# Layer 0's self-attention: turned probabilities between two projections, copied by one engine, scaled in two halves, and a new order of the first loads

## The chip, the core and the metric

The kernel is one program on one core of a Trainium2 chip. The core has five engines that run their own instruction queues in order and meet at semaphores: TensorE (PE in the profile; PEld is its loading of the stationary operand), VectorE (DVE), ScalarE (ACT), GpSimd (POOL) and SyncE (SP), which here only issues transfers. The metric is the device time of one execution in microseconds (us), as the median of several runs. Beside it stands one profiled execution with its trace; its span is the time from its first to its last instruction.

## What is computed

The reference is a decoder of two layers on 32 sequences of 100 tokens with 256 features, in float32. Each layer is self-attention, cross-attention to a context of 361 rows, and a mixture of experts, each on a layer norm of x and added to x. The change lies in layer 0's self-attention, and that is all that is needed here:

```
xn = layernorm(x)                                # 32 x 100 x 256
q, k, v = xn Wq + bq, xn Wk + bk, xn Wv + bv      # 16 heads of 64
p = softmax(causal(q k^T / 8))                    # 100 x 100 for each head
x = x + (p v) Wo + bo
```

After it come layer 0's cross-attention and experts, and then layer 1.

## The kernel before, in words

**Layout.** x stays in SBUF for the whole kernel: 3,200 rows as 25 tiles of 128 rows (NF = 25, D = 256). A normed and transposed copy, xnT, holds features on the partitions. A sequence has 100 rows, so tiles and sequences do not line up; `pieces` and `tile_of` map one to the other.

**Start.** SP issues, in this order: all of x in seven transfers (L91), the four weights wq, wk, wv, wo of 1 MB each into one tile wA (L243), the biases bqk, bv, bo (L247, L248, L134), and then fills and weight staging in DRAM for later stages (from L1097). SP has one queue, so what stands first goes first.

**Stage.** `l0_attn` runs 64 steps, n = 0 to 63, two for each sequence b, with eight heads each (g = n % 2). Two extra steps drain the pipeline. The order of TensorE's work is written out by hand (`manual_schedule` for PE); the order on the other engines is a scheduler's, which follows the data and its own estimate of times. Ahead of the loop stand `front(0)` and `front(4)` (norm and transposes of tiles 0 to 7), the projections of the first two sequences, and the first values.

In a step TensorE does, in this order:

- `scores(n)`: 8 products q k^T into two PSUM banks (16 matmul records in the profile, out of tiles qk). VectorE then copies the allowed ones into s (masked copy, L310) and takes the negative row maximum m (L312). ScalarE takes 8 exps with row sums rz (L316), VectorE the reciprocal of rz (L319), and GpSimd multiplies e by it, all 100 x 800 elements at once (L320).
- `proj` for q and then for k: an eighth of the projections of the next two sequences, two blocks of each. ScalarE adds q's bias (L287), VectorE k's (L289).
- `turn(n-1)`: 8 transposes of the probabilities of the step before, into two banks, copied out to sT by `evac` (L329).
- `vals(b+1, g)`: half of v for the next sequence; VectorE adds the bias (L297).
- `values(n-1)`: p v from sT and v; ScalarE copies the result to zT (L341).
- every now and then `out`: the output projection of a finished tile of 128 rows, added to x by VectorE (L230) with its norm statistics; in some other steps `front` or `next_norm`: norm and transposes of tiles (L200).

`evac` alternates by a counter that runs through the whole kernel: every second copy goes to ScalarE, the others to VectorE (in layer 1's cross-attention every third to ScalarE). In `turn` the first half goes to VectorE and the second to ScalarE.

All PSUM banks of this stage have one tag with 8 buffers, so each request takes the bank that was asked for eight requests earlier and waits for its readers. A step asks for eight: two for scores, one for q, two for turn, one each for k, v and values; `out`, `front` and `next_norm` ask for more.

In the last steps (n of 60 and more) there are no sequences left to project, so `turn` follows the scores directly.

Of the kernel before, what the change touches and what calls it, by code (L numbers as in the profile page):

```python
# [12 lines left out]
AF = mybir.ActivationFunctionType  # L13
ALU = mybir.AluOpType
AX = mybir.AxisListType

P = 128
NB = 32
T = 100
NT = NB * T  # L20
NF = NT // P
# [23 lines left out]
FRONT0 = {**{f: 4 for f in range(0, 20, 4)}, 20: 5}  # L45
# [32 lines left out]
class Kernel:  # L78
    def __init__(self, ctx, tc, a):
        self.ctx, self.tc, self.nc, self.a = ctx, tc, tc.nc, a  # L80
        nc = tc.nc
        self.n_evac = 0
        self.const = ctx.enter_context(tc.tile_pool(name="const", bufs=1))
        self.wts = ctx.enter_context(tc.tile_pool(name="wts", bufs=1))
        self.lnp = ctx.enter_context(tc.tile_pool(name="ln", bufs=2))
        self.norms, self.norm_of = {}, {}
        self.x = self.const.tile([P, NF, D], F32, tag="x", name="x_sb")
        xd = a["x"].rearrange("b t d -> (b t) d").rearrange("(f p) d -> p f d", p=P)
        for f in range(0, NF, 4):
            n = min(4, NF - f)  # L90
            nc.sync.dma_start(self.x[:, f : f + n, :], xd[:, f : f + n, :])  # L91
        self.xnT = self.const.tile([P, NK, NT], F32, tag="xnT", name="xnT")
        self.ident = self.const.tile([P, P], F32, tag="ident", name="ident")
        make_identity(nc, self.ident)
# [60 lines left out]
        return t  # L155


    def norm_stats(self, f, groups):

        nc = self.nc  # L160
        f0 = max(g for g in groups if g <= f)
        n, i = groups[f0], f - f0
        if i == 0:
            self.norm_of[n] = [
                self.lnp.tile([P, n, *k], F32, tag=f"{tag}{n}", name=tag)
                for tag, k in (("st", [6]), ("mv", [2]), ("rstd", []))
            ]
        st, mv, rstd = self.norm_of[n]
        self.norms[f] = mv[:, i, 0:1], rstd[:, i : i + 1]
        nc.vector.bn_stats(st[:, i, :], self.x[:, f, :])  # L170
        nc.vector.bn_aggr(mv[:, i, :], st[:, i, :])
        if i == n - 1:
            nc.vector.tensor_scalar_add(rstd, mv[:, :, 1], EPS)
            nc.scalar.activation(rstd, rstd, AF.Sqrt)
            nc.vector.reciprocal(rstd, rstd)
# [57 lines left out]
    def l0_attn(self):  # L233
        nc, tc, a = self.nc, self.tc, self.a
        with ExitStack() as st:
# [3 lines left out]
            wq, wk, wv, wo = (w[:, i * 2048 : (i + 1) * 2048] for i in range(4))  # L239
            wq, wk, wv = (v.rearrange("p (k n) -> p k n", k=NK) for v in (wq, wk, wv))  # L240
            wo = wo.rearrange("p (c n) -> p c n", c=8)
            for t, n in ((wq, "wq0"), (wk, "wk0"), (wv, "wv0"), (wo, "wo0")):
                nc.sync.dma_start(t, a[n].rearrange("(k p) n -> p k n", p=P))  # L243
            cp = st.enter_context(tc.tile_pool(name="c0a", bufs=1))
            pool = st.enter_context(tc.tile_pool(name="p0a", bufs=2))
            bqk = cp.tile([P, 2, 8], F32, tag="bqk", name="bqk")
# [2 lines left out]
            nc.vector.tensor_scalar_mul(bqk[:, 0, :], bqk[:, 0, :], 0.125)  # L249
            bv = self.row_bias(cp, a["bv0"], 1024, "bv")  # L250
            bo = self.row_bias(cp, a["bo0"], D, "bo")
            keep = self.tri(cp, "keep", -1, 1, 1.0, 0.0)
            mask = cp.tile([T, T], U32, tag="mask", name="mask")
            nc.vector.tensor_copy(mask, keep)
# [6 lines left out]
            q, k, v, p, sT = {}, {}, {}, {}, {}  # L261
# [3 lines left out]
            def front(f):  # L265

                n = FRONT0[f]
                for i in range(f, f + n):
                    self.norm_stats(i, FRONT0)
                for i in range(f, f + n, 2):  # L270
                    m = min(2, f + n - i)
                    self.norm_turn(i, m, self.norm_rows(i, m, bias=bo), self.bank_m())

            def proj(b0, c, ws, out, s):

                if c == 0:
                    out[b0 // 2] = pool.tile([P, 8, 2 * T], F32, tag=f"qk{s}", name=f"qk{s}")
                t = out[b0 // 2]
                pm = self.bank_m()[:, : 4 * T].rearrange("p (c t) -> p c t", c=2)
                for j in range(2):  # L280
                    self.mm(pm[:, j, :], [
                        (ws[:, i, (c + j) * P : (c + j + 1) * P], self.xn_of(i, b0, 2)) for i in range(NK)
                    ])
                for j in range(2):
                    bias = bqk[:, s, c + j : c + j + 1]
                    if s == 0:
                        nc.scalar.activation(t[:, c + j, :], pm[:, j, :], AF.Identity, bias=bias, scale=0.125)  # L287
                    else:
                        nc.vector.tensor_scalar_add(t[:, c + j, :], pm[:, j, :], bias)  # L289
# [10 lines left out]
            def scores(n):  # L300
                b, g = divmod(n, 2)
                cols = slice((b % 2) * T, (b % 2 + 1) * T)
                s = ss[n % 2]
                ps = [self.bank_s()[:T, : 4 * T].rearrange("p (c t) -> p c t", c=4) for _ in range(2)]
                for c in range(4):
                    for j in range(2):
                        r = slice(64 * j, 64 * j + 64)
                        self.mm(ps[j][:, c, :], [(q[b // 2][r, 4 * g + c, cols], k[b // 2][r, 4 * g + c, cols])])
                for j in range(2):
                    nc.vector.copy_predicated(s[:, 4 * j : 4 * j + 4, :], self.mid(mask, 4), ps[j])  # L310
                m = pool.tile([T, 8], F32, tag="m", name="m", bufs=3)
                nc.vector.tensor_reduce(m, s, AX.X, ALU.max, negate=True)  # L312
                t = p[n] = pool.tile([T, 8, T], F32, tag="e", name="e", bufs=3)
                rz = pool.tile([T, 8], F32, tag="rz", name="rz", bufs=3)
                for i in range(8):
                    nc.scalar.activation(  # L316
                        t[:, i, :], s[:, i, :], AF.Exp, bias=m[:, i : i + 1], accum_out=rz[:, i : i + 1]
                    )
                nc.vector.reciprocal(rz, rz)  # L319
                nc.gpsimd.tensor_tensor(t, t, self.last(rz, T), ALU.mult)  # L320

            def turn(n):
                t = p.pop(n)
                for j in range(2):
                    pt = self.bank_t()[:T, : 4 * T].rearrange("p (c t) -> p c t", c=4)
                    for c in range(4):
                        nc.tensor.transpose(pt[:, c, :], t[:, 4 * j + c, :], self.ident[:T, :T])
                    sT[n, j] = pool.tile([T, 4, T], F32, tag="sT", name="sT", bufs=4)
                    self.evac(sT[n, j], pt)  # L329

            def values(n):
                b, g = divmod(n, 2)
# [10 lines left out]
            def out(b):  # L343

                f = tile_of(b)
                if f is None:
                    return
                self.out_proj(f, wo)
                self.norm_stats(f, HALVES)
                if f in (5, 11, 17):  # L350
                    later.extend(range(f - 5, f, 2))
# [4 lines left out]

            with tc.manual_schedule(engines={mybir.EngineType.PE}):
                front(0)
                front(4)
                for c in range(0, 8, 2):  # L360
                    proj(0, c, wq, q, 0)
                    proj(0, c, wk, k, 1)
                for n in range(2):
                    vals(0, n)
                last = 2 * NB
                for n in range(last + 2):
                    b, g = divmod(n, 2)
                    if n < last:
                        scores(n)
                        b0 = b // 2 * 2 + 2  # L370
                        if b0 < NB:
                            c = 2 * (n % 4)
                            proj(b0, c, wq, q, 0)
                            proj(b0, c, wk, k, 1)
                    if 0 < n <= last:
                        turn(n - 1)
                    if b + 1 < NB:
                        vals(b + 1, g)
                    if 0 < n <= last:
                        values(n - 1)  # L380
                    if g:
                        if b > 0:
                            out(b - 1)
                    elif b % 5 == 4 and b < 20:
                        front(4 * (b + 6) // 5)
                    elif later:
                        next_norm()
# [1582 lines left out]
```

## Time and profile before

| | |
|---|---|
| median of 3 runs | 3237.91 us (3234.86 to 3237.93) |
| profiled execution, its time | 3232.65 us |
| its span | 3230.9 us |
| mean granted TensorE clock | 0.979 |
| head, 0 to 31 us: PE busy | 18.27 us |
| layer 0 self-attention, 31 to 620: PE, DVE, ACT, POOL busy | 559.6, 299.7, 308.0, 114.9 us |
| its steps begin | scores 0 at 31.19, scores 2 at 44.22, scores 60 at 577.56 |
| a plain step in it | 7.45 us; with an output projection 11.10 us |
| layer 0 cross-attention begins | 619.16 us |

How to read it: the page gives the busy time of each engine as a share of the span. A wait is given as engine, result and line, then whom it waited for, and then the total, the count and the longest wait in us. A line of the timeline gives start, duration, engine, line, operation, result and operands, shapes and count; in square brackets stands the idle time of that engine just before, and what ended it. Instructions of one kind that follow each other are merged into one line, so a gap inside such a line is seen only in its length. ps_t is a PSUM bank, whatever it holds. `x16` for scores are 8 products with two records each.

### The profile page before, as it was taken

To read this page: it belongs to the slowest core of one execution; us is meant where nothing else is said; L and a number is where in the kernel's file an instruction comes from. 1 tells how busy PE (TensorE), PEld (TensorE's weight loads), DVE (VectorE), ACT (ScalarE), POOL (GpSimd) and SP (SyncE) were. 2 spreads that over 40 slices of the span, in tenths; PEclk is the share of its full clock that TensorE was granted. 3 is DMA by queue.
4 is the path that set the end of the run, shared out by engine and by line. 5 is a ranking of instruction groups with operands and counts; after the bars stand their busy time and mean duration, and the time that the engine had idled before them with its cause. 6 is when DMAs were issued, how large, how long until landed. Compare 5 with 4: busy or idle time off the path is not lost. (4 is left out here: it accounts for less than half of the span.)

```text
span 3230.9 us, 67902 instructions
## 1 busy us (share of the span) xinstructions
PE 3076.5 (95%) x26832; PEld 2234.8 (69%) x26832; DVE 1773.6 (55%) x4565; ACT 1412.5 (44%) x4407; POOL 912.2 (28%) x984
## 2 busy tenths in 40 slices
PE   8999999899999999999997999999999999999983
PEld 6777777566666657888884677777777777776662
DVE  5555545466766742222225776667666676665442
ACT  4554555466566531122122225555555555555120
POOL 2211211255555543000006330011212112122474
PEclk9999999899999999999998999999999999999996
DMA  9830000000000022554452000000000000000486
GB/s 316 305 133 1 1 1 1 13 14 14 14 14 14 7 96 100 182 203 178 176 213 75 15 5 6 6 30 27 21 12 10 11 10 13 7 11 13 138 202 187
DMA packets 122440, 225.86 MB, mean 70 GB/s; under 512 B 40541, under 2 KB 98837, under 8 KB 115328
## 3 DMA queue, kind: packets, MB, share of 16 engines
q1 hardware_dynamic: 93600, 127.32, 12.3%
q0 software_dynamic: 27792, 90.81, 8.7%
q8 instruction: 215, 3.52, 0.5%
q10 hardware_dynamic: 720, 3.28, 0.2%
q14 instruction: 113, 0.93, 0.1%
HBM read 153.77 MB, written 113.61 MB: 83 GB/s over the span
## 5 line engine op out<-in xcount | busy, mean ns | idle before, releaser
L1628 POOL DMA_INDIRECT x_d<-xr,slot x200 | 194.4, 972 | 786.3 <-DVE kT L124 243.4
L425 ACT ACTIVATE wBx<-ps_t,m 100x361 f32<-100x361 f32 x512 | 281.0, 560 | 261.0 <-DVE m L422 238.6
L595 DVE TENSOR_REDUCE m<-ps_t 100x1 f32<-100x361 f32 x512 | 240.1, 525 | 109.6 <-PE ps_t L129 108.7
L129 PE MATMUL ps_t<-xnT,wA 128*128 128x200 f32 x1536 | 287.2, 337 | 3.0 <-DMA wA<-in_wq 1.5
L129 PEld LDWEIGHTS ps_t<-xnT,wA 128*128 128x128 f32 x1536 | 259.7, 190 | 38.7 <-issue 17.5
L422 DVE TENSOR_REDUCE m<-ps_t 100x1 f32<-100x361 f32 x512 | 241.4, 525 | 78.9 <-PE ps_t L129 76.9
L129 PE MATMUL ps_t<-xT,w 128*128 128x256 f32 x1276 | 283.2, 381 | 0.7 <-ACT xT L123 0.7
L129 PEld LDWEIGHTS ps_t<-xT,w 128*128 128x128 f32 x1276 | 240.0, 190 | 41.7 <-issue 9.3
L320 POOL TENSOR_TENSOR e<-e,rz 100x800 f32<-100x800 f32 x64 | 97.4, 1522 | 456.2 <-DVE rz L319 450.9
L129 PE MATMUL ps_t<-wA,cT 128*121 128x512 f32 x384 | 186.9, 598 | 5.3 <-DVE kT L124 5.3
L616 ACT ACTIVATE e<-ps_t 121x300 f32<-121x300 f32 x512 | 173.2, 431 | 41.7 <-PE ps_t L129 41.7
L129 PE MATMUL ps_t<-kT,qT 64*100 64x361 f32 x1024 | 190.2, 488 | 0.9 <-ACT wBx L425 0.9
L129 PE MATMUL ps_t<-cT,wA 128*128 128x361 f32 x512 | 189.8, 495 | 1.3 <-DVEq L1228 1.3
L316 ACT ACTIVATE e<-s,m 100x100 f32<-100x100 f32 x512 | 186.1, 365 | 5.9 <-DVE m L312 5.5
L434 PEld LDWEIGHTS ps_t<-ident,wBx 100*121 100x121 f32 x1536 | 178.3, 186 | 12.6 <-issue 5.5
L129 PE MATMUL ps_t<-wA,zT 128*128 128x256 f32 x800 | 185.4, 385 | 0.0
L434 PE MATMUL ps_t<-ident,wBx 100*121 100x100 f32 x1536 | 185.4, 270 | 0.0
L620 POOL TENSOR_TENSOR es<-e 121x400 f32<-121x400 f32 x128 | 132.6, 1036 | 177.6 <-ACT e L616 177.5
L1310 DVE TENSOR_TENSOR h<-ps_t,g 128x256 f32<-128x256 f32 x145 | 61.2, 424 | 199.4 <-ACT g L1309 199.4
L129 PEld LDWEIGHTS ps_t<-wA,zT 128*128 128x128 f32 x800 | 150.8, 192 | 28.4 <-issue 3.5
L124 DVE COPY eT<-ps_t 121x300 f32<-121x300 f32 x340 | 146.9, 461 | 31.3 <-PE ps_t L434 27.9
L452 PE MATMUL ps_z<-eT,v 121*64 121x100 f32 x3072 | 160.3, 253 | 0.0
(301 smaller groups left out, 5776.6 us busy)
## 6 DMA issues: line engine op xcount, KB each, us to landing
x_d<-fill SPq DMA_DIRECT2D x16, 1284.0 KB
we<-in_wexp SPq DMA_DIRECT2D x32, 384.0 KB
cT<-in_ctxT SPq DMA_DIRECT2D x64, 181.5 KB
xe<-x_d SPq DMA_DIRECT2D x32, 321.0 KB
xe_d<-zero SPq DMA_DIRECT2D x8, 1024.0 KB
xe<-xe_d SPq DMA_DIRECT2D x29, 256.0 KB
y_d<-y SPq DMA_DIRECT2D x29, 256.0 KB
w_d<-in_wg SPq DMA_DIRECT2D x16, 320.0 KB
```

The source lines that it names most:

```text
L124: return self.nc.vector.tensor_copy(out, in_)
L129: self.nc.tensor.matmul(out, lhsT=l, rhs=r, start=(i == 0), stop=(i == n - 1))
L316: nc.scalar.activation(t[:, i, :], s[:, i, :], AF.Exp, bias=m[:, i : i + 1], accum_out=rz[:, i : i + 1])
L320: nc.gpsimd.tensor_tensor(t, t, self.last(rz, T), ALU.mult)
L422: lay.after = nc.vector.tensor_reduce(m, ps[i], AX.X, ALU.max, negate=True)
L425: nc.scalar.activation(t[:, :L], ps[i], AF.Exp, bias=m, accum_out=sums[b][:, h : h + 1])
L434: nc.tensor.transpose(pt[:, c, :], e[n, i][:, c * KC : (c + 1) * KC], self.ident[:T, :T])
L452: nc.tensor.matmul(out, lhsT=v, rhs=eT[n, i][:, c, :], start=first, stop=last)
L595: nc.vector.tensor_reduce(m[:, j, o : o + 1], ps[r], AX.X, ALU.max, negate=True)
L616: nc.scalar.activation(t[:, r], ps[r].rearrange("p (c t) -> p c t", c=NKC), AF.Exp)
L620: nc.gpsimd.tensor_tensor(s, t[:, :, 0, :], t[:, :, 1, :], ALU.add)
L1628: got = nc.gpsimd.indirect_dma_start(out=self.x1_d[:, :], out_offset=bass.IndirectOffsetOnAxis(ap=slot[:, j, k : k + 1], axis=0), in_=xr[: ...
```

## The change

Five edits, all in layer 0's self-attention or ahead of it:

1. Of x, tiles 0 to 3 are loaded first, in two transfers; then wq and wk; then tiles 4 to 7; then the biases; then wv and wo; then the rest of x.
2. The statistics of tiles 4 to 7 may not start before the last normed row of tiles 0 to 3.
3. The scale by the reciprocal row sums is done in two halves of four heads, each with its own reciprocal. The first half can be scaled after four exps, the second after eight.
4. `turn` copies both halves out by VectorE; `evac` and its counter are not used. The counter stands 128 lower after this stage, so every second copy still falls to the same engine later, and every third one does not.
5. In a step, the projection for q comes before `turn` and the projection for k after it.

```diff
-        for f in range(0, NF, 4):
-            n = min(4, NF - f)
+        def load_x(f, n=4):
+            n = min(n, NF - f)
             nc.sync.dma_start(self.x[:, f : f + n, :], xd[:, f : f + n, :])
+        self.load_x = load_x
+        load_x(0, 2)
+        load_x(2, 2)
...
-        nc.vector.bn_stats(st[:, i, :], self.x[:, f, :])
+        got = nc.vector.bn_stats(st[:, i, :], self.x[:, f, :])
+        if after is not None:
+            self.depend(got, [after.ins], "not ahead of the first tiles' norm")
...
-            for t, n in ((wq, "wq0"), (wk, "wk0"), (wv, "wv0"), (wo, "wo0")):
+            for t, n in ((wq, "wq0"), (wk, "wk0")):
                 nc.sync.dma_start(t, a[n].rearrange("(k p) n -> p k n", p=P))
+            self.load_x(4)
...
             bo = self.row_bias(cp, a["bo0"], D, "bo")
+            for t, n in ((wv, "wv0"), (wo, "wo0")):
+                nc.sync.dma_start(t, a[n].rearrange("(k p) n -> p k n", p=P))
+            for f in range(8, NF, 4):
+                self.load_x(f)
...
-                    self.norm_stats(i, FRONT0)
+                    self.norm_stats(i, FRONT0, self.last_row if f == 4 else None)
...
-                for i in range(8):
-                    nc.scalar.activation(
-                        t[:, i, :], s[:, i, :], AF.Exp, bias=m[:, i : i + 1], accum_out=rz[:, i : i + 1]
-                    )
-                nc.vector.reciprocal(rz, rz)
-                nc.gpsimd.tensor_tensor(t, t, self.last(rz, T), ALU.mult)
+                for j in range(2):
+                    h = slice(4 * j, 4 * j + 4)
+                    for i in range(8)[h]:
+                        nc.scalar.activation(
+                            t[:, i, :], s[:, i, :], AF.Exp, bias=m[:, i : i + 1], accum_out=rz[:, i : i + 1]
+                        )
+                    nc.vector.reciprocal(rz[:, h], rz[:, h])
+                    nc.gpsimd.tensor_tensor(t[:, h, :], t[:, h, :], self.last(rz[:, h], T), ALU.mult)
...
-                    self.evac(sT[n, j], pt)
+                    nc.vector.tensor_copy(sT[n, j], pt)
...
                             proj(b0, c, wq, q, 0)
-                            proj(b0, c, wk, k, 1)
                     if 0 < n <= last:
                         turn(n - 1)
+                    if n < last and b0 < NB:
+                        proj(b0, c, wk, k, 1)
```

More of the change, by code (lines that the diff above doesn't have):

```diff
@@ L155, in tri, with norm_stats @@
         return t
-    def norm_stats(self, f, groups):
+    def norm_stats(self, f, groups, after=None):
         nc = self.nc
```

## The prediction

> **What bounds the kernel now.** I read the page first (shares by engine), then busy time by stage, then the waits of TensorE inside the stage that the diff touches, then that stage's timeline step by step.
>
> ```profile
> PE 3076.5 (95%) x26832; PEld 2234.8 (69%) x26832; DVE 1773.6 (55%) x4565; ACT 1412.5 (44%) x4407; POOL 912.2 (28%) x984
> ```
>
> The whole is TensorE-bound. Layer 0's self-attention lies at 31 to 620 us; there PE is busy 559.6 of 589 us. The waits of PE from 31 to 577, and from 577 to 620, are these:
>
> ```profile
> PE ps_t L129 <- ACT sT L123: 18.3, 33, 2.0
> ...
> PE ps_t L327 <- POOL e L320: 7.6, 2, 4.2
> PE ps_t L129 <- DVE sT L124: 1.2, 2, 0.9
> ```
>
> So the only thing the steady steps wait for is ScalarE's copy of turned probabilities. One such step in the timeline:
>
> ```profile
> 304.15 0.85 PE L327 MATMUL ps_t<-ident,e 100*100 100x100 f32 x8
> 304.84 1.88 PE L129 MATMUL ps_t<-wA,xnT 128*100 128x512 f32 x4
> 305.04 0.57 DVE L124 COPY sT<-ps_t 100x400 f32<-100x400 f32 x1
> ...
> 306.57 0.47 ACT L123 COPY sT<-ps_t 100x400 f32<-100x400 f32 x1
> 306.76 0.20 DVE L319 RECIPROCAL rz<-rz 100x8 f32<-100x8 f32 x1 [1.14 <-ACT e L316]
> 307.09 0.71 PEld L129 LDWEIGHTS ps_t<-sT,v 100*64 100x64 f32 x16 [1.21 <-ACT sT L123]
> 307.09 0.91 PE L129 MATMUL ps_t<-sT,v 100*64 100x100 f32 x16 [0.36 <-ACT sT L123]
> ```
>
> The transposes end at 305.0. VectorE copies its half at once, ScalarE its half only at 306.57, after the eighth exp of the next step, which stands ahead of it. The values matmul starts late.
>
> How much in all: start to start, a step's work on PE is scores 0.88, projections 2.81, turn 0.69, values of the next batch 1.81 (579.18 to 580.99, where nothing waits), weighted values 0.84: 7.03 us. The 58 steps from 44.22 to 577.56 take 533.3. Of that 58 x 7.03 = 407.7 is work, 22 output projections x 3.65 = 80.3, norm transposes 9.9 (nine of 0.59, three of 1.01, one of 1.54, read as differences between steps). 35.4 is left. A plain step loses 0.42 (551.56 to 559.01 is 7.45); part of it hides inside matmul groups that read 1.33 long in place of 0.91, so the waits view shows only 18.3. Steps with norm work lose up to 2.0.
>
> **What the Trainium skill says.** "TensorE: Matmul & The Clock Gate", under "Architectural detail": ScalarE and VectorE are strict FIFO. The trace agrees: the copy waited 1.6 us behind exps. Same page, Part 1: after an idle window of about 3.4 us the array runs at half clock until a busy one. The trace agrees:
>
> ```profile
> 584.00:586.00 2.00, 0.00 (x0) 0.00 (x0) 1.05 (x2) 1.18 (x7) 1.35 (x1) 1.00 0.00 0
> 586.00:588.00 2.00, 1.78 (x10) 1.22 (x11) 0.57 (x1) 2.00 (x13) 0.17 (x1) 0.76 0.00 0
> 588.00:590.00 2.00, 2.00 (x3) 0.30 (x2) 0.00 (x0) 0.82 (x4) 0.00 (x0) 0.50 0.00 0
> ```
>
> (columns: stretch, PE, PEld, DVE, ACT, POOL busy, clock, DMA). After 3.44 idle the clock is 0.50. "ScalarE: Activation LUTs", "What ACT_TABLE_LOAD costs": about 1.28 us per load; the trace has 1.28.
>
> **Part 1, copies and order.** Both copies go to VectorE, and the transposes move ahead of the k projection (1.405 us, half of 2.81), so they end at 0.88 + 1.405 + 0.69 = 2.97 us into the step instead of 4.38. VectorE's queue in the built program then is: two masked copies (0.98 to 2.08), max (to 3.07), two sT copies of 0.57 (to about 4.25), k bias add, reciprocal, add, reciprocal, v add. Weighted values stand at 7.03 - 0.84 = 6.19. The copies have 1.9 us to spare; the stall goes: -0.42 in a plain step. The new weight falls on VectorE: +0.57 and one more reciprocal of at most 0.20. Does it become the bound? Its loop: exps run from 3.17 (0.1 after the max) for 8 x 0.363 to 6.07; second reciprocal to 6.4; v add 0.64 to 7.05; next masked copy wanted at 7.03 + 0.98 = 8.0. Spare 0.95. In the steps with norm rows (up to four x 0.36) or a table load (1.28) the copies slip by 1.4 to 1.7, still under 1.9. Banks: eight are taken per step as before, and every bank that PE waits for was freed in the step before. What is late next: nothing; PE itself. I take -33.7 (35.4 less 1.75 below), with +1 for the tightest norm steps.
>
> **Part 2, the scale in halves.** GpSimd, not in the way: 100x800 takes 1.52, a 128x256 add 0.72, so 400 elements are estimated at 0.95 to 1.04. Second half ready at about 6.4 + 1.1 = 7.5; its transposes come at 7.03 + 2.28 + 0.35 = 9.66. Hidden by 2.1 us; uncovered it would cost +0.5 per step. The transposes now carry waits for single exps; the before's step 1 (36.70) carries seven such and turns in 0.73, so at most +0.04 a step if not overlapped, 0 taken. More ACT counting signals: no row, between 0 and +0.02 x 58; 0 taken.
>
> **Part 3, the clock.** At 198 to 201 the clock is 0.50 after a 1.65 us stall on sT; steps 188.27 and 198.72 lose 4.0 together where like steps lose 1.84 and 0.42: 1.75 is clock. Without the stall it should go: -1.75 (0 if it was not the stall).
>
> **Part 4, the tail (577.56 to 619.16).** No projections; PE waits for exps, scale, transposes. The second half of the scale alone is on that chain (-0.5 each time), but VectorE now puts its two sT copies around the max, where ScalarE had the first (+0.9 at two groups of values). By hand, from scores 60 at 0: masked copies to 2.2 (behind an output's add and stats, 1.0), sT to 2.8, max to 3.75, sT to 4.3, values end 5.1 (before 4.27); exps to 6.75, halves scaled at 6.4 and 8.0, turn ends 8.4 (before 9.4); vals, values, output end 14.7 (before 17.3, with 1.65 of half clock: vals 3.53 for 1.88); the next values end 19.9 (20.9), the next turn 23 (27.6), output 28.9 (35.0, half clock again), cross-attention begins 36.0 (41.6). So 5.6 earlier if the clock stays up. Idle pieces of 1 to 3 us remain, and the clock may dip in them as before, so I take about half: -3 (0 to -6).
>
> **Part 5, the head.** SP's order: x 0-3, wq, wk, x 4-7, biases, wv, wo, the rest. Before, x 0-3 are in at 5.07, wq at 15.5, wk at 18.05: 2.55 per 1 MB weight, 364 GB/s for x. Estimated: wq 7.6, wk 10.1, x 4-7 11.6, bq 12.5, x 8-11 20.4, last x 25. But PE's order keeps the transposes of tiles 4-7 ahead of the first projection. Their chain: stats, aggregates (0.39 a tile), with the bias scale queued between and waiting for bq, to 13.9; root and reciprocal 0.5; four rows; transposes 15.2 to 17 or, at half clock after some 6 us idle, 18.5. The 64 projection records (0.1756 each) then end at 28.2 to 30; before they end at 27.66 (1.4 + 0.9 waiting for wq and wk). Stats of tiles 8 to 24 now sit between k bias adds on VectorE, waiting for x; the root of tiles 20-24 sits between the first two groups of exps and costs two more table loads, 2.56, which the next exps start late by, with turn(1) still covered. Zero fills start after x in either order, same bytes ahead. The two smaller x transfers add one DMA to SP, 0.44 to 0.51 of issue, while the queue is full. Whether the array is really cold there the trace of before can't show: its first transposes (430 and 380 ns against 279 later) look cold though the clock reads 1.00. Sum: +2.5 at the start of step 2 (0 warm and early, +5 cold with x late).
>
> **Sum.** -33.7 + 1 - 1.75 - 3 + 2.5 = -35. Later stages keep their work; a different alternation of copies in the last cross-attention changes no wait of PE, which shows none there. Span 3230.9 - 35 = 3196. The profiled execution is 3232.65, 1.75 around the span, and 5.3 under the runs' median 3237.91, so the median becomes 3203.
>
> **Rivals.**
> 1. VectorE takes over: each in-order wait on it adds a bit and the loop grows from 6.1 to 7.25. Then only 0.2 of the 0.42 is won: 58 x 0.22 = 12.8 less: 3216. For: two reciprocals wait for exps with the v add behind. Against: 0.95 spare.
> 2. The head gives back more: x late, half clock through the projections: +10 in place of +2.5: 3211. Against: weights are all in by 10.
> 3. It does not do what it says: PE's time moves into another wait of equal size, such as the earlier transposes for the scale. They come 1.4 sooner. Against: 2.1 spare. About 3238.
> 4. Slower: the same loop on VectorE beyond 7.45, that is 1.3 us over my sum. At 7.7: 58 x 0.25 = 14.5, less the sum's small terms (-2): 3250. For: VectorE does all evacuation but qk and z. Against: its busy time per step is 4.3 + 0.8 of 7.
>
> **How the numbers follow.** Main case 0.70, own range 3193 to 3213 (head, tail and clock at their ends); rival 1 0.13; rival 2 0.08; rival 3 0.04; rival 4 0.05. Faster than 0.2% (6.5 us, what this kernel's runs can tell from no change): 0.91; within: 0.04; slower: 0.05. The range takes in rivals 1 and 2 with their own spread, and at its low end a tail without half clock: 3190 to 3222.
>
> **What would show it.** Right: no wait of PE for sT between 50 and 570; plain steps of 7.03 to 7.07; steps with an output at 10.7; the clock at 1.00 around 198; step 2's scores at 45 to 49; the tail's two clock dips shorter. Wrong: PE waiting for DVE in values or for POOL in turn (rivals 1, 3), masked copies starting later than 1.3 after the scores begin, projections later than 20 us (rival 2).

## The result and the profile after

The changed kernel takes 3204.05 us (median of 5 runs, 3193.76 to 3207.05); the kernel before, beside it, 3237.91. The ratio is 0.990, 95% interval 0.9884 to 0.9916: faster by 1.0%. A later set of runs of both gave 3201.19 against 3236.13, ratio 0.9896 (0.9875 to 0.9916). The forecast was 3203, with 3190 to 3222 around it.

The line of the page with TensorE's share, after:

```profile
span 3202.3 us, 68027 instructions
...
PE 3067.3 (96%) x26832; PEld 2231.9 (70%) x26832; DVE 1813.5 (57%) x4692; ACT 1393.2 (44%) x4346; POOL 925.7 (29%) x1048
```

The same number of matmuls is busy for 9 us less, and the span is 28.6 us shorter: 19 us of idle went, and 9 us by which waits inside a group or a halved clock had stretched matmuls. The waits of PE in the whole of steps 2 to 59 (50.3 to 549.7 us; total, times, longest) are now one line, and it is not about copies:

```profile
PE ps_t L207 <- DVE xn L185: 0.2, 1, 0.2
```

Before, this stretch had 18.3 us of waits for ScalarE's copy. One step in the timeline after, one with an output projection behind the values (start, length, engine and line, operation; PE, VectorE and GpSimd's first half scale):

```profile
313.96 0.95 PE L134 MATMUL ps_t<-qk,qk 64*100 64x100 f32 x16
...
314.85 1.62 PE L134 MATMUL ps_t<-xnT,wA 128*128 128x200 f32 x8
314.95 1.10 DVE L322 COPY_PREDICATED s<-mask,ps_t 100x400 f32<-100x400 uint32 x2 [0.94 <-PE ps_t L134]
316.08 0.99 DVE L324 TENSOR_REDUCE m<-s 100x8 f32<-100x800 f32 x1
...
316.30 0.85 PE L341 MATMUL ps_t<-ident,e 100*100 100x100 f32 x8
...
316.98 1.04 DVE L343 COPY sT<-ps_t 100x400 f32<-100x400 f32 x2
...
319.23 0.85 POOL L334 TENSOR_TENSOR e<-e,rz 100x400 f32<-100x400 f32 x1 [4.86 <-DVE rz L333]
...
320.18 0.91 PE L134 MATMUL ps_t<-sT,v 100*64 100x100 f32 x16
```

Both copies end at 318.02, 4.06 us into the step; the values matmul that reads them starts at 320.18, 6.22 in, with 2.2 to spare and no wait (in the steps with norm rows the room goes down to 0.75). PE is through with it at 321.02, 7.06 after the scores began.

From the same timeline, by the starts of the steps, the change is placed like this (us):

| stretch | before | after | change | predicted |
|---|---|---|---|---|
| start to step 2 | 44.22 | 50.29 | +6.07 | +2.5 |
| steps 2 to 59 | 533.34 | 499.42 | -33.92 | -34.45 |
| step 60 to the cross-attention's first matmul | 41.60 | 38.52 | -3.08 | -3 |
| from there to the end of the span | 2611.7 | 2614.1 | +2.3 | 0 |
| span | 3230.9 | 3202.3 | -28.6 | -35 |

The head is the part that went against the forecast. PE's first projection in the kernel before, and PE's timeline of the head after:

```profile
15.54 1.62 PE L129 MATMUL ps_t<-xnT,wA 128*128 128x200 f32 x8 [1.46 <-DMA wA<-in_wq]
```

```profile
6.87 1.99 PE L207 MATMUL ps_t<-ident,xn 128*128 128x128 f32 x8 [6.87 <-DVE xn L185]
17.09 0.48 PE L207 MATMUL ps_t<-ident,xn 128*128 128x128 f32 x1 [8.23 <-DVE xn L185]
17.82 1.21 PE L207 MATMUL ps_t<-ident,xn 128*128 128x128 f32 x4 [0.26 <-DVE xn L185]
19.28 0.90 PE L207 MATMUL ps_t<-ident,xn 128*128 128x128 f32 x3 [0.26 <-DVE xn L185]
19.98 12.84 PE L134 MATMUL ps_t<-xnT,wA 128*128 128x200 f32 x64
...
44.43 0.55 PE L341 MATMUL ps_t<-ident,e 100*100 100x100 f32 x4 [0.24 <-POOL e L334]
45.88 0.55 PE L341 MATMUL ps_t<-ident,e 100*100 100x100 f32 x4 [0.90 <-POOL e L334]
```

The first projection stands at 19.98 (15.54 before), behind the transposes of tiles 4 to 7, whose rows come late. And step 1 now waits 1.14 us for the two halves of the scale. Of the 6.07 us, 4.99 are there when step 0 begins (36.18 for 31.19), and step 1 adds 1.08 (8.60 for 7.52).

### The profile page after: what moved, and what is told of

Its sections match the earlier page's. It is cut to its first block, busy times and chain, and to the rows that moved or that the text cites. A ratio compares the mean times of both kernels' runs of the same rounds, so it can differ in the third digit from the quotient of the medians.

```text
span 3202.3 us, 68027 instructions
## 1 busy us (share of the span) xinstructions
PE 3067.3 (96%) x26832; PEld 2231.9 (70%) x26832; DVE 1813.5 (57%) x4692; ACT 1393.2 (44%) x4346; POOL 925.7 (29%) x1048
## 5 line engine op out<-in xcount | busy, mean ns | idle before, releaser
L134 PE MATMUL ps_t<-xnT,wA 128*128 128x200 f32 x1536 | 299.4, 339 | 0.6 <-DVE x_sb L237 0.6
L334 POOL TENSOR_TENSOR e<-e,rz 100x400 f32<-100x400 f32 x128 | 109.5, 856 | 414.0 <-DVE rz L333 397.1
L631 ACT ACTIVATE e<-ps_t 121x300 f32<-121x300 f32 x512 | 173.4, 430 | 41.7 <-PE ps_t L134 41.6
L129 DVE COPY eT<-ps_t 121x300 f32<-121x300 f32 x339 | 146.7, 461 | 31.2 <-PE ps_t L449 27.1
```

Source lines behind the costliest of these rows:

```text
L129: return self.nc.vector.tensor_copy(out, in_)
L134: self.nc.tensor.matmul(out, lhsT=l, rhs=r, start=(i == 0), stop=(i == n - 1))
L334: nc.gpsimd.tensor_tensor(t[:, h, :], t[:, h, :], self.last(rz[:, h], T), ALU.mult)
L631: nc.scalar.activation(t[:, r], ps[r].rearrange("p (c t) -> p c t", c=NKC), AF.Exp)
```

## The experiments

Each ratio is against runs of the kernel before on the same chip: its median is 3224.68 us on one chip and 3236 on two others, so medians of different chips are not compared. The starts of the steps come from each run's own profile; "cross-attention" is its first matmul (619.16 before, 588.23 after).

**The copies alone.** The theory to test: the copies carry the gain of the steps. The rival: the place of the transposes does, or the two share it.

```diff
 # kernel before
-                    self.evac(sT[n, j], pt)
+                    nc.vector.tensor_copy(sT[n, j], pt)
```

> The kernel before with one edit: both copies of turned probabilities on VectorE. My theory (the stall is ScalarE's copy standing behind eight exps, and the place of the transposes only adds room): in a plain step the transposes end 4.4 us in, VectorE's two copies run to about 5.5, the values matmul wants them at 6.19, so plain steps come down from 7.45 to 7.03-7.08 and out steps from 11.10 to 10.7. In steps with norm rows four rows of 0.36 can stand ahead of the copies, so some 0.5 stays in each of about 13 such steps: steps 2 to 59 take 500 to 508 us against 533.3, cross-attention begins 26 to 34 us earlier, head unchanged (step 2 at 44.2 +- 0.3). Rival A (the order is what pays, the copies alone only move the wait): plain steps at 7.3 or more, cross-attention at most 12 us earlier. Rival B (VectorE becomes the bound): plain steps above 7.45, no gain.

Ratio 0.9906 (0.9891 to 0.9922), 3193.81 against 3224.68. Plain steps 7.03, output steps 10.68, steps 2 to 59 in 498.90, step 2 at 44.05, cross-attention at 585.02: 34.1 earlier than in the kernel before and 3.2 earlier than in the changed one. The 0.5 us that I had left in each step with norm rows is mostly not there: seven of those steps take 7.62, which is 7.03 plus the 0.59 of the transposes. Its timeline shows the room (PE and VectorE only):

```profile
304.00 0.85 PE L327 MATMUL ps_t<-ident,e 100*100 100x100 f32 x8
304.21 0.76 DVE L289 TENSOR_SCALAR qk<-ps_t,bqk 128x200 f32<-128x200 f32 x2 [0.69 <-PE ps_t L129]
...
304.69 1.88 PE L129 MATMUL ps_t<-wA,xnT 128*100 128x512 f32 x4
...
304.88 1.04 DVE L329 COPY sT<-ps_t 100x400 f32<-100x400 f32 x2
...
306.51 0.91 PE L129 MATMUL ps_t<-sT,v 100*64 100x100 f32 x16
```

The scores of this step began at 300.31; the copies end 5.6 into it, 0.6 before the values matmul. That is less room than the 2.2 of the changed kernel, and in nearly every step it is enough: the waits view of steps 2 to 59 names sT no more. In three steps with norm rows on VectorE it is not quite, which that view doesn't show because the delay lies inside the group: the values matmuls there take 1.25 us once and 1.01 twice, for 0.91 (steps of 11.03 for 10.68 and 7.72 for 7.62).

**The transposes between the projections alone.**

```diff
 # kernel before
                             proj(b0, c, wq, q, 0)
-                            proj(b0, c, wk, k, 1)
                     if 0 < n <= last:
                         turn(n - 1)
+                    if n < last and b0 < NB:
+                        proj(b0, c, wk, k, 1)
```

> The kernel before with one edit: the transposes between the q and the k projection, copies still one on each engine. ScalarE's copy still stands behind the eight exps, which end about 6.07 us into the step, so it is done at 6.5 while the values matmul wants it at 6.19. My theory: plain steps stay at 7.40 to 7.50, cross-attention begins within 5 us of before's 619.2, the time within 0.2% of before. Rival (the transposes' lateness is what makes the copy late): plain steps at 7.05 to 7.2, 15 us or more gained.

Ratio 0.9999 (0.9991 to 1.0007). Plain steps 7.44 to 7.45, steps 2 to 59 in 530.21, cross-attention at 620.08. The waits of PE from 53 to 540 name the same line as before:

```profile
PE ps_t L129 <- ACT sT L123: 13.3, 24, 1.9
```

ScalarE's copy stands behind its eight exps whether the transposes come early or not: in the step at 299.63 they end at 302.8, and the copy starts at 305.73, after the eighth exp.

**All but the copies.** The changed kernel with the copies alternating again:

```diff
 # changed kernel
-                    nc.vector.tensor_copy(sT[n, j], pt)
+                    self.evac(sT[n, j], pt)
```

> The changed kernel with one copy of each pair back on ScalarE. My theory (the copies alone carry the gain of the steady steps): plain steps back at 7.40 to 7.50, steps 2 to 59 at 525 to 534 against 499.4, PE waiting for ScalarE's copy; the time 25 to 35 us over the changed kernel, ratio to before 0.998 to 1.003. Rival (the three edits of the body share the gain): steps 2 to 59 at 520 or less.

Ratio 1.0003 (0.9994 to 1.0013). Plain steps 7.42 to 7.46, steps 2 to 59 in 527.24, cross-attention at 620.67, and PE waits again for the same copy:

```profile
PE ps_t L134 <- ACT sT L128: 15.1, 25, 1.9
```

With the two before, this shows the gain of the steps to be the copies': alone they give all of it. Without them the other edits together give no measurable time in the whole, as two effects cancel. Steps 2 to 59 take 6.1 us less than in the kernel before, in six single late steps (the largest 10.71 for 12.52 and 10.70 for 12.27), and the last steps 1.7 less; but step 2 starts at 53.54, 9.3 later, with the new head and one wait of 1.72 for ScalarE's copy in step 1.

**The halves alone.**

```diff
 # kernel before
+                for j in range(2):
+                    h = slice(4 * j, 4 * j + 4)
+                    for i in range(8)[h]:
...
-                nc.vector.reciprocal(rz, rz)
-                nc.gpsimd.tensor_tensor(t, t, self.last(rz, T), ALU.mult)
+                    nc.vector.reciprocal(rz[:, h], rz[:, h])
+                    nc.gpsimd.tensor_tensor(t[:, h, :], t[:, h, :], self.last(rz[:, h], T), ALU.mult)
```

> The kernel before with one edit: the scale of the probabilities in two halves. My theory (the scale is hidden in the steady steps by some 2 us and bare only in the last four): plain steps stay at 7.43 to 7.50 with PE waiting for ScalarE's copy as before, steps 2 to 59 take 532 to 536, and only the last steps gain: 37.5 to 40 from step 60 to the cross-attention in place of 41.6; the time within 0.2% of before. Rival (the scale carries part of the steady stall): plain steps under 7.35, 6 us or more gained in steps 2 to 59.

Ratio 0.9985 (0.9976 to 0.9993): a small gain, 4.3 us in the medians. Plain steps 7.44 to 7.47, step 60 to cross-attention 40.01 for 41.60, and steps 2 to 59 in 536.69, just over what I gave. Two output steps account for it: 14.19 where the kernel before has 12.52, and 12.70 where it has 11.10. Busy time by stretch around the first (stretch, its length, PE, PEld, DVE, ACT, POOL busy, granted clock, DMA share, GB/s):

```profile
112.00:114.00 2.00, 0.56 (x13) 0.54 (x13) 0.76 (x2) 1.41 (x7) 1.53 (x2) 1.00 0.81 253
114.00:116.00 2.00, 2.00 (x13) 1.62 (x9) 0.00 (x0) 0.49 (x1) 0.18 (x1) 0.70 0.77 235
116.00:118.00 2.00, 2.00 (x6) 1.56 (x6) 0.00 (x0) 0.00 (x0) 0.00 (x0) 0.50 0.65 184
```

A wait of 1.44 us for sT ends at 113.47, and the clock goes to 0.50. In the kernel before, the same step waits 1.46 and keeps its clock. So a wait of this size may or may not cost the clock. In the ten profiles of kernels that copy on VectorE alone, the clock never goes down between step 2 and step 60. As this profile's cross-attention begins 2.3 us later than before (621.46), the gain of the medians isn't placed: the 1.6 of the last steps are part of it, the rest stays open.

**The scale whole again in the changed kernel.**

```diff
 # changed kernel
-                for j in range(2):
-                    h = slice(4 * j, 4 * j + 4)
-                    for i in range(8)[h]:
...
-                    nc.vector.reciprocal(rz[:, h], rz[:, h])
-                    nc.gpsimd.tensor_tensor(t[:, h, :], t[:, h, :], self.last(rz[:, h], T), ALU.mult)
+                nc.vector.reciprocal(rz, rz)
+                nc.gpsimd.tensor_tensor(t, t, self.last(rz, T), ALU.mult)
```

> The changed kernel with the scale put back to one instruction per unit. The kernel with the copies alone ran plain steps of 7.03 where the changed one runs 7.05. Theory H (the halves cost this, by more signals and waits): plain steps 7.03, steps 2 to 59 at 498 to 499; theory O (the transposes between two projections cost it): 7.05 as in the changed kernel, 499.4. Both: the end of the stage loses what the halves gave, 41 to 43 from step 60 to the cross-attention against 38.5, and step 1 to 2 grows from 8.6 to about 9, since the transposes there wait for the whole scale; the cross-attention begins 1 to 4 us later than in the changed kernel.

Ratio 0.9921 (0.9902 to 0.994). Plain steps stay at 7.05 to 7.06, steps 2 to 59 at 499.69: theory O. The 0.02 us a step come from the transposes standing between two projections, not from more signals; the old head below keeps 7.05 too, so they aren't the head's either. Step 60 to cross-attention is 41.89, as expected. What I had too small is the first turn: step 1 takes 11.30, for 8.60 with halves. PE there:

```profile
42.50 1.62 PE L134 MATMUL ps_t<-xnT,wA 128*128 128x200 f32 x8
46.49 1.44 PE L339 MATMUL ps_t<-ident,e 100*100 100x100 f32 x8 [2.38 <-POOL e L332]
47.73 2.71 PE L134 MATMUL ps_t<-xnT,wA 128*128 128x200 f32 x8
```

The wait for the scale (44.92 to 46.44) doubles, and the group after it takes 2.71 where 1.54 is usual: the clock reads 0.50 from 46.7 to 50.1. So with the transposes early, the halves are worth 2.7 us in step 1 (1.2 of wait, the rest mostly clock) and 3.4 at the end, and next to nothing between.

**The old head.** The changed kernel with the loads and first norms of the kernel before:

```diff
 # changed kernel
-        load_x(0, 2)
-        load_x(2, 2)
+        for f in range(0, NF, 4):
+            n = min(4, NF - f)
+            nc.sync.dma_start(self.x[:, f : f + n, :], xd[:, f : f + n, :])
...
-            for t, n in ((wq, "wq0"), (wk, "wk0")):
+            for t, n in ((wq, "wq0"), (wk, "wk0"), (wv, "wv0"), (wo, "wo0")):
                 nc.sync.dma_start(t, a[n].rearrange("(k p) n -> p k n", p=P))
-            self.load_x(4)
...
-            for t, n in ((wv, "wv0"), (wo, "wo0")):
-                nc.sync.dma_start(t, a[n].rearrange("(k p) n -> p k n", p=P))
-            for f in range(8, NF, 4):
-                self.load_x(f)
...
-                    self.norm_stats(i, FRONT0, self.last_row if f == 4 else None)
+                    self.norm_stats(i, FRONT0)
```

> The changed kernel with the loads and the first norms put back as in the kernel before. My theory: the load order cost the 5 to 6 us by which step 2 is late in the changed kernel (50.3 against 44.2), so step 2 starts at 43.5 to 45.5, steps 2 to 59 take 499.4 +- 1 as in the changed kernel, cross-attention begins at 581 to 584 (588.2 in the changed kernel, 619.2 before), and the kernel is 4 to 7 us faster than the changed one, ratio to before about 0.988. Rival (the halves and the earlier transposes delay the first steps whatever the loads): step 2 at 47 or later, gain under 3 us.

Ratio 0.9888 (0.9871 to 0.9905). First projection 15.54, step 2 at 44.87, steps 2 to 59 in 499.42, cross-attention at 581.42: 5.4 us of step 2's delay are the new head's. The start has a spread of its own: step 0 begins at 31.2 to 32.9 in the six profiles with the old head, and at 36.1 to 37.3 in the four with the changed kernel's. The interval of the ratio overlaps that of the changed kernel, so the whole time doesn't show the difference.

**Tiles 4 to 7 off the first projections' way.**

```diff
 # changed kernel
                 front(0)
-                front(4)
...
                 for n in range(2):
                     vals(0, n)
+                front(4)
```

> The changed kernel with one edit: the transposes of tiles 4 to 7 behind the first projections and the first values instead of ahead of them. My theory (the new head loses because the first projection stands behind tiles whose data lands at 14.1 us, though the weights are in by about 11): the first projection starts at 9.5 to 12 in place of 19.98, step 2 at 40 to 46 in place of 50.3, cross-attention begins 4 to 10 us earlier than in the changed kernel, ratio to before about 0.988. Against it: three square roots now stand between the first groups of exps with two table loads of 1.28 us each, which may give 2 to 4 us of it back in steps 1 to 4. Rival (the projections wait for the key weights or the biases as long as for the tiles): first projection or its evacuation at 17 or later, no gain over the changed kernel.

Ratio 0.9879 (0.9861 to 0.9897). Ahead of the projections PE now waits for the query weights:

```profile
10.45 12.80 PE L134 MATMUL ps_t<-xnT,wA 128*128 128x200 f32 x64 [1.57 <-DMA wA<-in_wq]
```

The first projection is at 10.45 in place of 19.98. The q projection's first result is evacuated only at 15.45: its scaled bias stands on VectorE behind the statistics of tile 4, which wait for data until 14.53. This doesn't hold PE back. Step 2 starts at 41.49, steps 2 to 59 take 500.20, and the cross-attention begins at 581.88.

**Tiles 4 to 7 loaded one place earlier.**

```diff
 # changed kernel
             for t, n in ((wq, "wq0"), (wk, "wk0")):
                 nc.sync.dma_start(t, a[n].rearrange("(k p) n -> p k n", p=P))
-            self.load_x(4)
+                if t is wq:
+                    self.load_x(4)
```

> The changed kernel with the load of tiles 4 to 7 one place earlier, ahead of the key weights. My theory (the late first projection is the late landing of these tiles, 14.1 us): they land one weight transfer, about 2.5 us, earlier, at 11.3 to 12; the first projection starts at 16.8 to 18 in place of 19.98, and step 2 at 47 to 48.5 in place of 50.3. Rival (the norm of these tiles waits for something else, the bias scale queued on VectorE or GpSimd): first projection at 19 or later.

3199.01, ratio 0.9884 (0.986 to 0.9908). The tiles are there at 11.44 (14.10 before this edit), the first projection starts at 17.02, step 2 at 45.95, cross-attention at 584.32. Step 2 is earlier than I gave, because the 64 projections take 12.02 for 12.84 (six of them run at half pace, for eleven in the changed kernel) and step 1 8.05 for 8.60.

**The parts that pay, put together.** Copies on VectorE; transposes after both projections, as before; halves only in the last four units (the scores of steps 60 to 63); the new loads, with tiles 4 to 7 behind the first projections.

```diff
 # changed kernel
-                for j in range(2):
-                    h = slice(4 * j, 4 * j + 4)
+                w = 4 if n >= 2 * NB - 4 else 8
+                for j in range(0, 8, w):
+                    h = slice(j, j + w)
...
                 front(0)
-                front(4)
...
                     vals(0, n)
+                front(4)
...
                             proj(b0, c, wq, q, 0)
+                            proj(b0, c, wk, k, 1)
                     if 0 < n <= last:
                         turn(n - 1)
-                    if n < last and b0 < NB:
-                        proj(b0, c, wk, k, 1)
```

> A version put together from the runs: both copies on VectorE, transposes after both projections as in the kernel before, the scale in halves only in the last four units, the new load order with the transposes of tiles 4 to 7 behind the first projections. Theory: step 2 at 40 to 41.5, steps 2 to 59 at 498.5 to 500, 37 to 40.5 from step 60 on, cross-attention at 576 to 582, the time 8 to 12 us under the changed kernel, ratio to before 0.985 to 0.988. Rival (table loads and waiting tiles take the head's gain back): cross-attention at 582 or later, no better than the changed kernel with the old head.

Ratio 0.9883 (0.9863 to 0.9904), just past the slow edge of what I gave; step 2 at 42.01, a little late, steps 2 to 59 in 498.93, cross-attention at 578.23. Then beside the changed kernel itself, on one chip, with a variant that keeps the old head:

> The changed kernel once more, on the same chip as the next three. Ratio to before 0.9885 to 0.9915; step 2 at 49.5 to 53, steps 2 to 59 at 499.4 +- 0.5, cross-attention at 586 to 592.

> The version put together from the runs (copies on VectorE, transposes where they were, halves in the last four units only, new load order with the transposes of tiles 4 to 7 behind the first projections), beside the changed kernel on one chip. Theory: cross-attention at 576 to 582, 8 to 12 us under the changed kernel, ratio to before 0.9855 to 0.988. Rival (the first steps and the clock in the last ones take it back): under 4 us better than the changed kernel.

```diff
 # variant with the old head: kernel before
-                    self.evac(sT[n, j], pt)
+                    nc.vector.tensor_copy(sT[n, j], pt)
...
+                w = 4 if n >= 2 * NB - 4 else 8
+                for j in range(0, 8, w):
+                    h = slice(j, j + w)
...
```

> The kernel before with two edits: both copies on VectorE, and the scale in halves in the last four units only. Theory: step 2 at 44.1, steps 2 to 59 at 498.9, 37.5 to 40 from step 60 to the cross-attention, which begins at 580 to 583; 5 to 9 us under the changed kernel, within 4 us of the put-together version with the new head. Rival (the head's order matters more than step 2's start shows, by the later loads): 8 us or more behind that version.

| kernel | median us | ratio (95%) | step 2 | steps 2 to 59 | cross-attention |
|---|---|---|---|---|---|
| changed | 3201.19 | 0.9896 (0.9875 to 0.9916) | 50.28 | 499.43 | 588.13 |
| put together, new head | 3194.36 | 0.987 (0.9848 to 0.9892) | 41.41 | 498.90 | 577.10 |
| put together, old head | 3196.08 | 0.9883 (0.9862 to 0.9904) | 44.66 | 498.90 | 581.98 |

Up to the cross-attention, the version put together is 11.0 us ahead of the changed kernel; of the whole time 6.8 is seen, between theory and rival. The intervals of the two ratios overlap, but both carry the spread of the kernel before; set beside each other, all five runs of the version put together (3189.74 to 3199.90) lie under all five of the changed kernel (3200.23 to 3205.84). So the stage is shown to be shorter, and a gain in the whole is seen on this chip, with its size uncertain. The variant with the old head is 5.1 under the changed kernel, as given. The two heads differ by 4.9 us at the cross-attention and by 1.7 us in the medians, which these runs do not tell from nothing.

## Why the prediction was right, and where it was wrong

**Part 1, steps.** Right in size and cause: -33.92 for -34.45 (with the clock); plain steps 7.05, output steps 10.71, no wait for sT. The copies end 4.06 us into the step shown for the 4.25 worked out. What wasn't right is the credit given to the move of the transposes: the copies alone gain as much and more (498.90 for 499.42). The move bought room (2.2 us for 0.6) of which only the three steps had use that the copies alone leave 0.10 to 0.34 us late, at a price of 0.02 in every step. The prediction bounded that 0.02 as the price of more signals; the run with the whole scale puts it on the order.

**Part 2, halves.** Taken at nothing in the steps: right. The place where the cover is gone, step 1, was missed: the prediction looked at turn(1), the transposes of step 2, and called them covered, but not at those of step 1. The exps start late there: the masked copies of step 0 begin 2.02 us after its scores, behind statistics on VectorE, for 0.99 in a plain step. The transposes come early, and PE waits 1.14 us even with halves, 2.38 without.

**Part 3, clock.** Steps 18 and 19, at 188.27 and 198.72 before, fell from 22.72 to 18.78 us together, 3.94 for the 4.0 worked out. The stretch at 198 before, and the stretches around 198 after:

```profile
198.00:200.00 2.00, 2.00 (x18) 1.67 (x18) 1.97 (x5) 0.58 (x1) 0.05 (x1) 0.50 0.14 25
```

```profile
196.00:198.00 2.00, 2.00 (x17) 1.96 (x17) 1.97 (x4) 0.75 (x2) 0.00 (x0) 1.00 0.19 39
198.00:200.00 2.00, 2.00 (x9) 1.07 (x7) 1.54 (x5) 1.72 (x9) 0.00 (x0) 1.00 0.11 25
```

The dip need not follow the wait, though: with the copies alternating in the changed kernel, the same step waits 1.62 us and keeps its clock. So the 1.75 was there to win in this profile of the kernel before, and not in every one.

**Part 4, tail.** -3.08 for -3. The waits moved as worked out: those for the scale fell from 7.6 to 2.4 us, and those for VectorE's copies rose from 1.2 to 3.1 (549.7 to 589 us after):

```profile
PE ps_t L134 <- DVE sT L343: 3.1, 6, 1.0
PE ps_t L341 <- POOL e L334: 2.4, 4, 0.8
```

The reason to take only half of the 5.6 held too, for one dip of the clock remains where there were two:

```profile
566.00:568.00 2.00, 0.39 (x3) 0.19 (x2) 2.00 (x4) 0.14 (x1) 0.00 (x0) 1.00 0.00 0
...
570.00:572.00 2.00, 1.07 (x6) 0.58 (x4) 1.58 (x4) 1.29 (x8) 1.54 (x2) 0.50 0.00 0
```

PE is busy 0.39 of the 2 us from 566, waiting for VectorE's copies; the clock is 0.50 from 570 to 580. Where the dips fall and how long they last differs: profiles of kernels with this same tail took 36.8 to 40.2. So the cause is right, and that the number is so close is in part luck. Without halves the tail is 41.6 to 42.7.

**Part 5, head: the step that failed.** I gave +2.5 (0 to +5) for the start of step 2; it is +6.07, outside the bounds. Three terms were too small.
- Tiles 4 to 7 were estimated in at 11.6, from 2.55 us a weight and 364 GB/s for x. They are in at 14.10; put one transfer earlier, at 11.44. What came late is the first weight: with these tiles off the way, PE gets the query weights at 10.45, where 7.6 was counted, and the tiles come 4.1 behind them, as counted (4.0). From 4 to 8 us the loads move 257 GB/s in the changed kernel and 360 in the kernel before; why is open. The chain from the tiles to the first projection, 5.88 us, is as long as I had it (5.4 warm, 6.9 cold), so the projections start at 19.98 for 17.0 to 18.5. That "weights are all in by 10" was said against rival 2 and is wrong for the same reason.
- The price of a cold array was put on the transposes alone. The projections paid as well: 12.68 us to their end for the 11.24 counted. This part is a matter of chance too: in the profile of the kernel before the projections pay nothing for it, but with its head and the transposes moved they take 13.87, and step 0 begins at 32.90 for 31.19.
- Step 1's wait for the scale, 1.14, was left out (Part 2).

With the old head step 2 starts at 44.87, and with the tiles off the way at 41.49, which is 2.7 before the kernel before: the rest of the new order cost nothing.

**The sum.** The span fell by 28.6 for 35: 3.6 of the gap are the head, 0.5 the steps, 2.3 the later stages, whose work is as it was. From the cross-attention to the end, the profiles of all these kernels range from 2597 to 2622 us, in no order that follows the edits; the chip seems to have more to do with it, as all four profiles from the chip with the fastest kernel before are at 2597 to 2603, and all others at 2605 or more. That the median came out at 3204.05 for 3203 is luck, because two errors cancel. I added to the changed kernel the 5.3 us by which the profiled run of before lay under its median; the profiled run of the changed kernel is its median. The stage shows 31 us of the 34 in the medians; the other 3 are inside what the later stages vary by, and stay unplaced.

**The rivals.** VectorE did not take over: plain steps 7.05. Rival 2 was right in kind but smaller: +6, not +10. The sign named for it, projections later than 20 us, stands at its edge: 19.98 here and 20.15 in the later profile. No new wait in the steps, and nothing slower.

## What to carry to other kernels

When PE waits for an evacuation, look first at what stands ahead of that one instruction in its engine's queue. Moving the copy to the queue that is free at that time gave all that the steps gained here; making its input earlier, with the queue unchanged, left plain steps at 7.44 to 7.45 and the whole time as it was. And loading weights first is worth something only if PE's written order can use them: here the first projection still stood behind tiles that the new order had made late.

## What the runs showed of the hardware

A granted clock of 1.00 in the first stretches of a profile can be no reading at all. After 8.23 us of idle in the head of the changed kernel, these stretches touch 8 projection matmuls in 2 us, then 14:

```profile
22.00:24.00 2.00, 2.00 (x8) 2.00 (x7) 0.00 (x0) 0.75 (x2) 0.00 (x0) 1.00 1.10 348
24.00:26.00 2.00, 2.00 (x14) 2.00 (x13) 1.10 (x3) 0.00 (x0) 0.00 (x0) 1.00 1.12 384
```

The first twelve projections start 0.33 us apart, and from 23.86 us on the distance is 0.17. The trace's first clock record stands at 23.73 us, and the view shows 1.00 where there is none. In all twelve profiles whose projections begin at the slow pace, the first record lies within 0.2 us of the change of pace, so the slow matmuls are best read as half clock that has no record. The 64 projections take 12.84 us here, for 64 x 0.1756 = 11.24 at the steady rate: 1.6 us that the clock column doesn't show. How many projections run slowly differs between these profiles, from 6 to 18.

The length of a wait alone doesn't tell whether the clock falls, and the 3.4 us of idle that the prediction reckoned with are not needed for it. In the steps, a wait of 1.44 us (halves alone) and one of 1.65 (before, ahead of 198) were followed by half clock; one of 1.46 and two of 1.96 (before, at 344 and 491) were not.

VectorE's norm rows can take twice as long. In the changed kernel's head, VectorE has

```profile
6.31 1.38 DVE L185 TENSOR_SCALAR xn<-x_sb,mv,rstd 128x256 f32<-128x256 f32 x4
...
16.62 2.61 DVE L185 TENSOR_SCALAR xn<-x_sb,mv,rstd 128x256 f32<-128x256 f32 x4
```

and GpSimd, beside the second of these,

```profile
16.15 5.71 POOL L200 TENSOR_TENSOR x_sb<-x_sb,bo 128x256 f32<-128x256 f32 x8 [11.27 <-DVE rstd L180]
```

A row is 0.41 us at 6.31, with GpSimd at rest, and up to 0.82 while its bias adds run. The run with tiles 4 to 7 loaded one place earlier moved the adds away: there they start at 16.03, and the four rows of the same tiles, which start at 14.68 to 15.73, take 0.41 each. In the 14 profiles up to 640 us, every row longer than 0.45 us (116 of 638) lies beside GpSimd work, and no row without such work beside it is longer than 0.42. So the doubling is shown to come with GpSimd's work and to go where that work is moved away; not every row beside it is longer (the first at 16.62 takes 0.41). The Trainium skill, "Advanced Engine Details and Errata", "Mode Summary", says that VectorE's second SBUF port is shared with GpSimd, and that GpSimd's instructions and VectorE's two-port ones block each other; the rows agree with it, but that it is this port no run shows.
